# Ten unread transposes of the identity in each step of a graph-attention kernel

## The chip, the cores and the metric

The kernel runs on one core of one Trainium2 chip, as one launch. The metric is the device time of that launch in microseconds; lower is better.

## The reference

One layer of graph attention over 12500 nodes of 256 features and 200000 edges, sorted by destination, with 8 heads of 32:

```python
h = relu(layernorm(x))
q, k, v = h @ Wq + bq, h @ Wk + bk, h @ Wv + bv          # 8 heads of 32
logits = einsum('ehd,ehd->eh', q[dst], k[src]) / sqrt(32)
expv = exp(logits - segment_max(logits, dst)[dst])
attn = expv / segment_sum(expv, dst)[dst]
agg = segment_sum(attn[:, :, None] * v[src], dst)
y = h + gelu(agg + h @ Wskip + bskip)
out = x + layernorm(y) * gamma + beta
```

All arrays are float32.

## The kernel before

The kernel first normalises all nodes and writes two tables to memory, h and the joined keys and values (`kv_tab`, line 349 makes them). It also plans the edges: they are cut into 8 streams, and each stream into tiles of 128 edges. From about 250 us on, a loop over steps `c` does the edges; each step handles three tiles (`K = 3`) of each of the 8 streams (`S = 8`), 3072 edges. There are 64 steps. The loop has 63 passes, `c` from 0 to 62; 62 of them run the full body, and the last, `c == NST - 2`, takes a branch of its own and leaves the loop, and the work after it ends the kernel.

What one step does, with the lines of the profile:

- `gather` and `gather_row` (L1492, L1504): GpSimd fetches the rows of `kv_tab` of the edges' sources, one indirect DMA for each tile and stream.
- `windows`, `turn_windows` (L1466 transposes, L1470 copy) and `queries` (L1480, L1484, copy L1487): the rows of h of the destinations, turned, and multiplied by Wq, give the queries of the nodes.
- `hot_e` (matmul L1529, activation L1532) and `hot_n` (L1542, L1545): matrices of ones and zeros that say which edge belongs to which node, in the two directions.
- `spread` (L1555): TensorE spreads the nodes' queries over the edges, into PSUM. `times` (L1566) multiplies them by the keys on VectorE, `total` (L1573) sums over each head: the logits, 64 for each of 128 edges.
- `turn` (L1592): TensorE transposes a tile's logits into a bank of PSUM. `maxima` scans them in both directions for the maximum of each node (L1604, L1605), subtracts it (L1607) and takes exp on ScalarE (L1608). `turn_back` (L1614) transposes the three tiles of weights back.
- `weights` (L1626, L1629) copies the weights of tiles 1 and 2; `weigh` (L1640, L1646) multiplies the values by the weights on VectorE.
- `add_up` (L1663): TensorE sums the weighted values of each node, for three groups of streams; ScalarE copies the sums (L1676), carries the last node's on to the next step's tile (L1680), and SyncE stores them (L1686).
- A `Pair` of node blocks (L1197 to L1320) is finished beside the steps from step 15 on: skip connection, gelu, layer norm, output. The object `Dense` (L1823 to L1878) takes, from step 2 to 50, the edges whose destination is among the first 16 nodes, without gathers; its `turn` is L1831, its `back` L1862.

The order of instructions on each engine is the order in which the program writes them: `keep` hangs each instruction behind the one before it on the same engine, without a semaphore. `turns`, called right after certain matmuls, issues the next waiting gather behind the latest TensorE instruction, with a wait for it:

```python
def turns(behind, n=1):
    for _ in range(n):
        if waiting:
            gather_row(*waiting.pop(0), behind)
```

The bank of the logits is one tile for all steps but the last, of 128 partitions by 512 columns:

```python
logits = xt_ps.tile([P, 512], F32, name="ps_x")

def weight(c, j):
    at = (0, K * P, K * P + SH)[j]
    return step[c]["xt"][:, at:at + SH]
```

`turn` writes partitions 0 to 63 of columns 0 to 383, one tile of 128 columns at a time; the forward scan writes partitions 64 to 127 of the same columns. `turn_back` writes all 128 partitions of columns 0 to 63 (tile 0), 384 to 447 (tile 1) and 448 to 511 (tile 2); `SH` is 64.

The order of the work around the two places of the change: before `turn_back(c)` come, on TensorE, the third tile's `turn(c, 2)`, the dense part's `logits`, the rest of `add_up(c - 1, 0)`, `add_up(c - 1, 1)`, `pair.turn()` and `add_up(c - 1, 2)`; behind it `hot_n(c, 0)`, `hot_n(c, 1)` and `spread(c + 1, 1, 0)`. The last TensorE work of a step is `spread(c + 1, 2, 1)`, `hot_e(c + 2, 2)`, the first two tiles of `add_up(c, 0)` and `hot_e(c + 2, 3)`; the next step begins there with the dense part's `turn`, `shifted` of the pair before (L1299, L1302), two spreads, `turn_windows(c + 2, 0)` and the turn of the third tile.

At the kernel's start 18 transposes of the identity are issued in the same way (L281, `WARM = 18`), ahead of the first work of TensorE.

Of the kernel before, what the change touches and what calls it, by code (L numbers as in the profile page):

```python
# [44 lines left out]
P = 128  # L45
# [6 lines left out]
K = 3  # L52
# [18 lines left out]
SIDE, FOUR = 2, 4  # L71
ONCE = (2, 51)
START, WARM = 4, 18
LANDED, GATHERED, ASIDE, LATER = 2, 4, 12, 14
PAD = 127.0

# [7 lines left out]
def gnn_kernel(ctx: ExitStack, tc: tile.TileContext, x, src, dst, Wq, bq, Wk, bk, Wv, bv,  # L84
# [380 lines left out]
    with tc.If(fits > 0) as branch:  # L465
        table = dram.tile([S, NT, SUMS], F32, name="table")
        walk_streams(tc, N, HID, NST, KL, many, ident, idx, d0_row, slot_row, near, near_n, e_tab, pen_tab,
                     h_tab, kv_tab, table, x, out, w_q, w_s, one_row, b_q3, b_s3, b_o3,
                     gam, beta, eps, run_tab, cnt_tab, own, Wk, bk, Wv, bv)
# [643 lines left out]
def walk_streams(tc, N, HID, NST, KL, many, ident, idx, d0_row, slot_row, near, near_n, e_tab, pen_tab, h_tab,  # L1113
# [7 lines left out]
    nc = tc.nc  # L1121
# [15 lines left out]
    def behind(ins, name):  # L1137

        tc.add_manual_dep(ins.ins, name, mybir.DependencyInfo(
            mybir.DependencyClass.NoSync, mybir.DependencyReason.DATA), reason="kept order")  # L1140

    def keep(ins):

        before = latest.get(ins.ins.engine)
        if before is not None:
            behind(ins, before)
        latest[ins.ins.engine] = ins.ins.name
        return ins
# [231 lines left out]
    with ExitStack() as es:  # L1380
# [41 lines left out]
        def tiles_of(c):  # L1422
            return KL if c == NST - 1 else K
# [14 lines left out]
        def penalties(c):  # L1438

            g = step[c]  # L1440
            g["pen"] = early.tile([P, CH + 1], BF16, name="pen", bufs=2)
            keep(nc.sync.dma_start(g["pen"], bass.AP(
                tensor=pen_tab.tensor, offset=pen_tab.offset + c * 2 * S * (CH + 1),
                ap=[[CH + 1, 2 * S], [0, HEADS], [1, CH + 1]])))
# [66 lines left out]
# [5 lines that stand above are left out]
# [8 lines left out]
        def hot_e(c, i):  # L1524

            if i == 0:
                step[c]["to_e"] = hot.tile([P, S // 2, CH], F32, name="to_e")
            ps = hot_ps.tile([P, S * WN], F32, name="ps_hot")
            keep(nc.tensor.matmul(ps[:, :CH], near[:, i * P:(i + 1) * P], step[c]["et"],  # L1529
                                  start=True, stop=True))  # L1530
            turns(latest[PE], (1, 0, 0, 2)[i])
            keep(nc.scalar.activation(step[c]["to_e"][:, i, :], ps[:, :CH], AF.Relu, scale=-1.0,  # L1532
                                      bias=ones))

        def hot_n(c, j):

            n = near_n.shape[1]
            if j == 0:
                step[c]["to_n"] = (hot.tile([P, K, n], F32, name="to_n", bufs=1) if c < NST - 1
                                   else done[0].spare(n)[:, None, :])  # L1540
            ps = hot_ps.tile([P, S * WN], F32, name="ps_hot")[:, :n]
            keep(nc.tensor.matmul(ps, step[c]["et"][:, j * P:(j + 1) * P], near_n, start=True,  # L1542
                                  stop=True))
            turns(latest[PE], (1, 0, 1)[j])
            keep(nc.scalar.activation(step[c]["to_n"][:, j, :], ps, AF.Relu, scale=-1.0,  # L1545
                                      bias=ones))
# [30 lines left out]

        logits = xt_ps.tile([P, 512], F32, name="ps_x")

        def weight(c, j):  # L1580

            at = (0, K * P, K * P + SH)[j]
            return step[c]["xt"][:, at:at + SH]
# [26 lines left out]
        def turn_back(c):  # L1610
            g = step[c]

            for j in range(tiles_of(c)):
                keep(nc.tensor.transpose(weight(c, j), g["W"][:, j * P:(j + 1) * P],  # L1614
                                         ident[:SH, :SH]))
# [5 lines left out]
        def weights(c, streams=slice(0, S)):  # L1621

            g = step[c]
            if "vw" not in g:
                products(c)
            keep(nc.scalar.copy(wden[c % 2][0:1, streams],  # L1626
                                g["kv"][0][0:1, streams, HID - HEADS:HID]))
            for j in range(1, tiles_of(c)):
                keep(nc.scalar.copy(g["vw"][j][:, :, :HEADS],  # L1629
                                    weight(c, j).rearrange("p (s h) -> p s h", s=S)))  # L1630

        def weigh(c, j, streams=slice(0, S), engine=None):
            g = step[c]
            t = g["vw"][j][:, streams]
            if engine:
                wj = t[:, :, :HEADS]
            else:
                engine = nc.vector
                wj = weight(c, j).rearrange("p (s h) -> p s h", s=S)[:, streams]
            keep(engine.tensor_tensor(  # L1640
                t[:, :, HEADS:].rearrange("p s (h d) -> p s h d", h=HEADS),
                wj[:, :, :, None].to_broadcast([P, t.shape[1], HEADS, D]),
                g["kv"][j][:, streams, HID:].rearrange("p s (h d) -> p s h d", h=HEADS),
                op=OP.mult))
            if j == 0:
                keep(engine.tensor_tensor(t[:, :, :HEADS], wj, wden[c % 2][:, streams],  # L1646
                                          op=OP.mult))
# [361 lines left out]
        for c in range(NST - 1):  # L2009
# [108 lines left out]
            if a:  # L2118
                a.top()
                a.exps()  # L2120
            turn_back(c)
            hot_n(c, 0)
            weights(c)
# [68 lines left out]
            add_up(c, 0, range(K - 1))  # L2192
            penalties(c + 2)
            hot_e(c + 2, 3)
            before, pair = pair, pair_next
            if c > 1:
                step[c - 2] = None
# [484 lines left out]
```

## Time and profile before

| | |
|---|---|
| time, median of 3 runs | 2711.11 us (2701.12 to 2712.65) |
| the profiled execution's own time | 2722.66 us |
| its span, first to last instruction | 2721.1 us |
| mean granted TensorE clock | 0.833 |
| busy: TensorE, VectorE, ScalarE, GpSimd | 77%, 70%, 44%, 58% of the span |
| transfers | 589.91 MB, mean 217 GB/s |

In the lines of the profile, PE is TensorE's matmuls, PEld its weight loads, DVE VectorE, ACT ScalarE, POOL GpSimd and SP SyncE. A row of a group gives the line of the kernel, the engine, the operation, the tiles written and read with their shapes, the number of instructions, then the busy time, the mean duration of one in ns, and the idle time of that engine just before these instructions with what ended it. A row in order of time gives the start, the duration, the same names, and in brackets the idle time before it. A row of waits gives the waiting instruction, what released it, the sum in us, how often, and the longest. A row of a stretch gives its length, then the busy time and number of instructions of PE, PEld, DVE, ACT and POOL, the granted clock of TensorE (1.00 is full), the busy share of the DMA engines, and GB/s. "issue" stands where the profile shows nothing that was waited for.

### The profile page before, as it was taken

To read this page: it belongs to the slowest core of one execution; us is meant where nothing else is said; L and a number is where in the kernel's file an instruction comes from. 1 tells how busy PE (TensorE), PEld (TensorE's weight loads), DVE (VectorE), ACT (ScalarE), POOL (GpSimd) and SP (SyncE) were. 2 spreads that over 40 slices of the span, in tenths; PEclk is the share of its full clock that TensorE was granted. 3 is DMA by queue.
4 is the path that set the end of the run, shared out by engine and by line. 5 is a ranking of instruction groups with operands and counts; after the bars stand their busy time and mean duration, and the time that the engine had idled before them with its cause. 6 is when DMAs were issued, how large, how long until landed. Compare 5 with 4: busy or idle time off the path is not lost. (4 is left out here: it accounts for less than half of the span.)

```text
span 2721.1 us, 38398 instructions
## 1 busy us (share of the span) xinstructions
PE 2093.9 (77%) x10881; PEld 1272.9 (47%) x10881; DVE 1915.3 (70%) x2373; ACT 1204.8 (44%) x2789; POOL 1591.6 (58%) x1744
## 2 busy tenths in 40 slices
PE   9994667776777778877878877787887777767776
PEld 4443444444444445544544444454554444444444
DVE  8885666666676667767766776666777766777776
ACT  5652233332334445445444544444545444444444
POOL 5457466666666556555555655555555555666664
PEclk9997688888788788878887887878888878887778
DMA  9777566766767677767777777767777776777774
GB/s 351 293 273 220 155 200 207 211 206 207 204 209 214 204 215 224 214 208 232 220 210 206 224 213 208 221 204 207 224 221 212 224 213 203 220 225 222 222 214 113
DMA packets 275205, 589.91 MB, mean 217 GB/s; under 512 B 60643, under 2 KB 133400, under 8 KB 272038
## 3 DMA queue, kind: packets, MB, share of 16 engines
q0 software_dynamic: 125344, 409.89, 51.4%
q1 hardware_dynamic: 148416, 176.36, 20.5%
q8 instruction: 89, 1.46, 0.2%
q10 hardware_dynamic: 1222, 1.11, 0.1%
q14 instruction: 134, 1.10, 0.1%
HBM read 505.52 MB, written 81.63 MB: 216 GB/s over the span
## 5 line engine op out<-in xcount | busy, mean ns | idle before, releaser
L1504 POOL DMA_INDIRECT kv<-kv_tab,idx x1472 | 1401.8, 952 | 981.9 <-issue 335.9
L1555 PE MATMUL ps_qe<-qw,to_e 64*128 64x256 f32 x3040 | 589.3, 501 | 34.1 <-DVE kv L1566 25.4
L1566 DVE TENSOR_TENSOR kv<-ps_qe,kv 128x1024 f32<-128x1024 f32 x380 | 451.5, 1217 | 147.2 <-remote 91.4
L1555 PEld LDWEIGHTS ps_qe<-qw,to_e 64*128 64x128 f32 x3040 | 403.5, 249 | 126.6 <-issue 45.5
L1640 DVE TENSOR_TENSOR vw<-ps_x,kv 128x2048 f32<-128x2048 f32 x188 | 427.0, 2271 | 49.7 <-ACT vw L1629 16.6
L1573 DVE TENSOR_REDUCE L<-kv 128x64 f32<-128x2048 f32 x190 | 433.9, 2283 | 4.8
L1484 PE MATMUL ps_hot<-w_q,hwT 128*128 128x256 f32 x768 | 251.3, 475 | 18.5 <-issue 9.9
L1663 PE MATMUL ps_a<-vw,to_n 128*32 128x264 f32 (+1 forms) x2232 | 228.4, 435 | 44.6 <-issue 25.3
L1532 ACT ACTIVATE to_e<-ps_hot,ones 128x384 f32<-128x384 f32 x256 | 146.9, 581 | 255.1 <-remote 96.9
L1487 ACT COPY qw<-ps_hot 128x256 f32<-128x256 f32 (+1 forms) x128 | 60.6, 474 | 344.0 <-PE ps_hot L1484 113.4
L1484 PEld LDWEIGHTS ps_hot<-w_q,hwT 128*128 128x128 f32 x768 | 165.6, 230 | 86.3 <-ACT hwT L1470 34.0
L1663 PEld LDWEIGHTS ps_a<-vw,to_n 128*32 128x32 f32 (+1 forms) x2232 | 88.7, 125 | 245.9 <-issue 194.3
L349 PE MATMUL ps_kv<-w_kv,hT 128*128 128x512 f32 x392 | 184.3, 593 | 0.7 <-ACT hT L263 0.7
L1420 ACT ACT_TABLE_LOAD x142 | 182.2, 1283 | 2.6
L1529 PE MATMUL ps_hot<-et,near 48*128 48x384 bf16 x256 | 94.1, 368 | 102.1 <-issue 84.8
L1614 PE MATMUL ps_x<-ident,W 64*128 64x64 f32 x189 | 28.9, 270 | 179.4 <-ACT hT L1222 113.9
L1470 ACT COPY hwT<-ps_hot 128x256 f32<-128x256 f32 (+1 forms) x128 | 61.2, 478 | 233.7 <-PE ps_hot L1466 129.5
L1604 DVE TENSOR_TENSOR_SCAN ps_x<-pen,ps_x 64x384 f32<-64x384 bf16 x63 | 60.6, 961 | 147.6 <-PE ps_x L1592 79.2
L1866 DVE TENSOR_TENSOR kv<-ps_hot,kv 128x256 f32<-128x256 f32 x49 | 20.8, 425 | 181.1 <-PE ps_hot L1862 100.3
L1680 ACT COPY kv<-ps_a 1x264 f32<-1x264 f32 x372 | 137.3, 369 | 4.5
L1545 ACT ACTIVATE to_n<-ps_hot,ones 128x384 f32<-128x384 f32 x189 | 108.6, 576 | 62.8 <-PE ps_hot L1542 44.9
L1614 PEld LDWEIGHTS ps_x<-ident,W 64*128 64x128 f32 x189 | 19.2, 161 | 210.6 <-ACT hT L1222 132.0
(437 smaller groups left out, 3029.3 us busy)
## 6 DMA issues: line engine op xcount, KB each, us to landing
kv<-kv_tab,idx POOLq DMA_INDIRECT x1520
kv_tab<-kvo SPq DMA_DIRECT2D x23, 1024.0 KB
hw<-h_tab SPq DMA_DIRECT2D x256, 64.0 KB
table<-sums_w SPq DMA_DIRECT2D x252, 61.9 KB
kv<-h_tab SPq DMA_DIRECT2D x98, 128.0 KB
sums<-table SPq DMA_DIRECT2D x94, 132.0 KB
h<-h_tab SPq DMA_DIRECT2D x94, 128.0 KB
x_f<-in_x_dram SPq DMA_DIRECT2D x94, 128.0 KB
```

The lines of the kernel that those rows point to most:

```text
L349: nc.tensor.matmul(ps_kv, hT[:, c, :], w_kv[:, c, :], start=c == 0, stop=c == KC - 1)
L1420: keep(nc.scalar.activation(dummy[:, 1:2], dummy[:, 0:1], function))
L1484: keep(nc.tensor.matmul(ps[:, b, :], g["hwT"][:, b, k, :], w_q[:, k, :], start=False, stop=k == KC - 1, skip_group_check=True))
L1504: ins = nc.gpsimd.indirect_dma_start(out=t[:, s, :], out_offset=None, in_=kv_tab[:, :], in_offset=bass.IndirectOffsetOnAxis(ap=idx[:, s, j ...
L1532: keep(nc.scalar.activation(step[c]["to_e"][:, i, :], ps[:, :CH], AF.Relu, scale=-1.0, bias=ones))
L1545: keep(nc.scalar.activation(step[c]["to_n"][:, j, :], ps, AF.Relu, scale=-1.0, bias=ones))
L1555: keep(nc.tensor.matmul(ps[:, b, a, :], g["to_e"][r, 2 * half + a, j * P:(j + 1) * P], g["qw"][r, (half + a) * half, :], start=True, stop= ...
L1566: keep(nc.vector.tensor_tensor(k, g["qe", half].rearrange("p b a d -> p a b d"), k, op=OP.mult))
L1573: keep(nc.vector.tensor_reduce(g["L"][:, j, :].rearrange("p (s h) -> p s h", s=S), g["kv"][j][:, :, :HID].rearrange("p s (h d) -> p s h d" ...
L1640: keep(engine.tensor_tensor(t[:, :, HEADS:].rearrange("p s (h d) -> p s h d", h=HEADS), wj[:, :, :, None].to_broadcast([P, t.shape[1], HEA ...
L1663: keep(nc.tensor.matmul(ps[at:at + w, :], g["to_n"][:, j, i * P + at:i * P + at + w], g["vw"][j][:, s, :], start=j == 0, stop=j == tiles_o ...
L1680: keep(copy(step[c + 1]["kv"][0][0:1, s, HID - HEADS:], ps[at:at + 1, :]))
```

## The change

A constant `IDLE = 5` and a function `idle(at, n)` are added. It issues `n` transposes of the 128 x 128 identity into columns `at` to `at + 127` of the bank of the logits, all 128 partitions. Nothing reads what they write. It is called twice in the loop's full body: with columns 384 to 511 ahead of `turn_back(c)`, and with columns 256 to 383 at the step's end, behind `hot_e(c + 2, 3)`. Both calls are in the body that the last pass leaves before. Nothing is removed or moved.

```diff
+IDLE = 5
...
         logits = xt_ps.tile([P, 512], F32, name="ps_x")
+
+        def idle(at, n):
+
+            for _ in range(n):
+                keep(nc.tensor.transpose(logits[:, at:at + P], ident, ident))
...
             if a:
                 a.top()
                 a.exps()
+            idle(K * P, IDLE)
             turn_back(c)
             hot_n(c, 0)
             weights(c)
...
             add_up(c, 0, range(K - 1))
             penalties(c + 2)
             hot_e(c + 2, 3)
+            idle((K - 1) * P, IDLE)
             before, pair = pair, pair_next
```

## The prediction

> **What bounds the kernel now.** I read the page's head first, then the groups by line, then stretches of time for the granted clock, then one step in order of time. The head says that no engine is full:
>
> ```profile
> span 2721.1 us, 38398 instructions
> PE 2093.9 (77%) x10881; PEld 1272.9 (47%) x10881; DVE 1915.3 (70%) x2373; ACT 1204.8 (44%) x2789; POOL 1591.6 (58%) x1744
> PEclk9997688888788788878887887878888878887778
> ```
>
> TensorE is the busiest, and its clock stands at seven to eight tenths after the first 200 us. Cutting the span into stretches of 3.4133 us, laid on the instants at which the clock changes, shows what the tenths are made of: each stretch is wholly at 1.00 or wholly at 0.50. The columns are the length, busy time of PE, PEld, DVE, ACT, POOL, then the clock.
>
> ```profile
> 1497.57:1500.99 3.42, 3.08 (x26) 1.57 (x22) 3.38 (x6) 1.34 (x4) 2.05 (x3) 1.00 0.73 232
> 1500.99:1504.40 3.41, 0.77 (x8) 0.75 (x10) 2.32 (x2) 2.82 (x9) 1.90 (x2) 1.00 0.67 191
> 1504.40:1507.81 3.41, 3.41 (x16) 2.33 (x14) 1.25 (x2) 2.70 (x9) 2.26 (x3) 0.50 0.71 209
> ...
> 1524.88:1528.29 3.41, 1.47 (x17) 0.70 (x10) 3.38 (x5) 0.80 (x2) 1.41 (x2) 1.00 0.85 275
> 1528.29:1531.71 3.42, 3.00 (x7) 1.66 (x8) 1.35 (x3) 2.31 (x6) 1.90 (x2) 0.50 0.47 122
> 1531.71:1535.12 3.41, 3.41 (x17) 2.24 (x16) 0.40 (x1) 0.00 (x0) 0.94 (x1) 0.50 0.34 100
> 1535.12:1538.53 3.41, 3.41 (x29) 1.92 (x28) 2.87 (x5) 2.11 (x6) 2.63 (x3) 1.00 0.65 171
> 1538.53:1541.95 3.42, 2.20 (x18) 1.19 (x16) 3.35 (x5) 1.36 (x5) 1.81 (x3) 1.00 0.76 237
> 1541.95:1545.36 3.41, 1.83 (x15) 1.33 (x15) 1.67 (x1) 3.34 (x12) 2.19 (x3) 1.00 0.65 182
> 1545.36:1548.77 3.41, 3.12 (x13) 2.19 (x12) 2.20 (x2) 1.98 (x4) 1.89 (x2) 0.50 0.77 235
> ...
> 1562.43:1565.84 3.41, 1.67 (x18) 0.51 (x17) 1.24 (x2) 1.16 (x2) 2.15 (x3) 1.00 0.82 252
> 1565.84:1569.25 3.41, 1.82 (x6) 1.05 (x7) 2.45 (x4) 1.62 (x5) 1.90 (x2) 0.50 0.68 195
> 262.00:2650.00 2388.00, 1817.24 (x9804) 1125.96 (x9805) 1663.75 (x1681) 1034.97 (x2408) 1405.15 (x1476) 0.82 0.72 212
> ```
>
> A full-clock stretch in which PE is busy for 0.77, 1.47, 1.83 or 1.67 us is followed by a half-clock one; after 2.20 us it is not. And half clock ends only after a stretch that is busy from end to end (3.41 of 3.41; after 3.00 it stayed). The same cut from 262 us on has 137 such falls (the first after 265.36, the last after 2630.80). Nineteen in twenty had under 1.85 us busy; of the 312 stretches after which the clock stayed full, the least busy twentieth begins below that. So the border lies near 1.5 to 1.8 us in 3.41. A clock of 0.82 over 2388 us is 2388 x 2 x 0.18 = 860 us at half clock, 6.3 us a fall, about two falls in each step of some 39 us.
>
> What half clock costs I take from whole steps, from one forward scan of the logits (L1604) to the next:
>
> ```profile
> 1177.61:1219.13 41.52, 33.79 (x170) 20.48 (x169) 28.34 (x31) 19.11 (x44) 22.52 (x24) 0.75 0.70 206
> 1413.39:1454.94 41.55, 33.66 (x170) 20.08 (x169) 28.33 (x31) 19.11 (x44) 23.03 (x24) 0.75 0.71 206
> 1296.48:1334.93 38.45, 30.19 (x170) 18.95 (x169) 28.32 (x32) 18.80 (x44) 22.42 (x25) 0.87 0.76 220
> 2014.75:2054.71 39.96, 30.64 (x170) 19.36 (x169) 28.27 (x32) 18.79 (x44) 22.96 (x25) 0.87 0.73 214
> ```
>
> The instructions are the same, 170 matmuls. At 0.75 a step has 41.5 x 0.5 = 20.8 us at half clock and takes 41.5 us; at 0.87 it has about 10.2 and takes 38.5 to 40.0, with 38.9 the mean of the twelve such steps between 858 and 2171 us. So (41.5 - 38.9) / (20.8 - 10.2) = 0.25 us of step for each us at half clock. PE is nearly always busy in half-clock stretches, so the most it could be is 0.5; half of the slowness reaches the step's end, half lies beside DVE, ACT and the gathers.
>
> **Where the two groups of transposes land.** PE alone, in order of time, one step:
>
> ```profile
> 1537.10 1.56 PE L1663 MATMUL ps_hot<-vw,to_n 128*64 128x264 f32 x12
> 1538.59 0.66 PE L1219 MATMUL ps_hot<-ident,h 128*128 128x128 f32 x4
> 1539.17 1.56 PE L1663 MATMUL ps_a<-vw,to_n 128*64 128x264 f32 x12
> 1543.18 0.40 PE L1614 MATMUL ps_x<-ident,W 64*128 64x64 f32 x3 [2.45 <-ACT hT L1222]
> ...
> 1525.41 0.33 PE L1529 MATMUL ps_hot<-et,near 48*128 48x384 bf16 x1
> 1525.69 0.66 PE L1831 MATMUL ps_hot<-ident,kv 128*128 128x128 f32 x4
> 1528.70 0.58 PE L1299 MATMUL ps_hot<-b_o,one_row 3*128 3x512 bf16 x1 [2.36 <-ACT to_e L1532]
> ```
>
> The group ahead of turn_back (call it A) follows the last L1663 of add_up(c - 1, 2) and stands in the wait of L1614. The one at the step's end (B) follows the last L1529 of hot_e(c + 2, 3) and stands ahead of L1831 (the dense part's turn) and L1299.
>
> **Price of a transpose.** The same instruction, identity into PSUM, stands at the kernel's start; L1219 and L1831 are the same form in the loop.
>
> ```profile
> 2.74 3.73 PE L281 MATMUL ps_t<-ident 128*128 128x128 f32 x18 [2.74 <-POOL ident masks.py:199]
> L281 PE MATMUL ps_t<-ident x18: 272/421/476, 2.7 to 6.2; 128*128 128x128 f32 x18
> L1614 PE MATMUL ps_x<-ident,W 64*128 64x64 f32 x189 | 28.9, 270 | 179.4 <-ACT hT L1222 113.9 <-issue 36.6 <-ACT W L1608 28.9
> PE ps_hot L1831 <- issue: 46.3, 22, 3.9
> PE ps_hot L1299 <- issue: 25.1, 18, 3.0
> PE ps_hot L1831 <- DMA hw<-h_tab: 15.3, 7, 2.6
> PE ps_hot L1299 <- ACT to_e L1532: 11.9, 7, 3.4
> ```
>
> Four L1219 take 0.66 us, one alone 0.27 (the least that L281 shows), so the second to fourth start 0.13 us apart on average; 0.11 where nothing holds the weight load. The L281 group, mostly at half clock, runs 18 in 3.73: 0.2 each. Five thus cost 0.55 us at full clock and 1.05 at half. The loop's full body runs for 62 steps (the last pass leaves before either place): 620 transposes, 620 weight loads.
>
> **Group A** is costed at nothing: L1614 waits 179.4 us in all, some 3 us a step, for exp(W) on ACT (behind the copy of L1222), and 0.55 to 1.05 us fits into it. Without that cover it would be 62 x 0.55 = 34 us. Its columns, 384 to 511, were last read by weigh(c - 1, 2) and by the copies of L1629, for which the matmuls of add_up just before it have waited, so no new wait for VectorE arises; turn_back writes them next, on the same engine.
>
> **Group B** delays whatever PE does next. The four rows of waits above are 54 waits and 98.6 us, mean 1.8, so in about 54 of 62 steps there is a wait, ahead of L1831 or right behind it ahead of L1299, that takes up the 0.55 us. In the other 8 the delay goes on to the spreads (L1555) and the turn of the last tile (L1592), for which the scan L1604 waits: 8 x 0.55 = 4.4 to 8 x 1.05 = 8.4 us, taken as 8, since the step's end is often at half clock. With no cover it would be 34 to 65 us. Its columns, 256 to 383, were last read by L1607 half a step earlier. No gather is hung on these transposes: the gathers' turns are taken from a matmul issued right before each call, and none of those calls follows either group directly. SP, POOL and ACT issue nothing new. PE's instruction stream grows by 1240 on some 21,800; I see no wait that I can put on its fetch.
>
> **What it saves.** The transposes add busy time at the front of both gaps. In the stretches quoted: B at 1525.74 to 1526.3, with L1831 pushed behind it into the gap, brings 1.47 to 2.0 us, above the border, so the 6.8 us at half clock from 1528.29 would go. B at 1564.8 brings 1.67 to 2.2. But A begins at 1500.66, of which 0.2 us falls into the stretch with 0.77: it stays below. And A at 1540.7 falls into the stretch that was busy enough already. The fall after 1514.64 (0.69 us busy) is of a third gap, ahead of L1466, that gets nothing. I did this for every stretch from 300 to 2650 us, pushing what follows B until a gap takes it up. With the border anywhere from 0.37 to 0.43 of a stretch, 11 to 16 of 135 falls rise above it; with a border of 0.46 to 0.5, 6 to 8. I take 16, as a stretch that climbs over the border is mostly one where the clock would have recovered late. 16 x 6.3 us x 0.25 = 25 us; by the most that half clock can cost (0.5), 50 us; with 6 falls, 9 us.
>
> **Sum.** -25 + 8 + 0 = -17 us. The profiled execution took 2722.66 us (span 2721.1), so 2705; the median of the runs, 2711.11, is 11.5 lower, so 2694. One chosen border decides a third of this. A change of 0.5% is 13.6 us, about what a measurement of this kernel can tell from none.
>
> [...] In the first stretch of the kernel PE runs nothing but transposes (L281), and their durations fall from 476 ns to 272 within the group, with nothing else on PE: transposes open the clock here. [...]
>
> **Rivals.**
> (1) *Nothing is saved.* Either transposes open the clock but do not hold it, or each fall that is avoided comes back one gap later, for instance in the third gap, or PE's regained time ends in DVE's and the gathers' waits. For it: some 120 of 137 falls are untouched even by my count, and the spread between steps at 0.87 (38.45 and 39.96) is as large as what one fall is worth. Against: the regular 41.5 us of every step at 0.75. Time: 2711 + 0 to 8, 2715.
> (2) *Slower, by group A: late reports of PE's work.* ACT's copy of the sums of add_up(c - 1, 1) needs the twelve L1663 that end at 1538.66, and starts only when the later L1663, which it doesn't need, are through:
>
> ```profile
> 1541.06 0.38 ACT L1676 COPY sums_w<-ps_hot 128x264 f32<-128x264 f32 x1 [2.01 <-PE ps_a L1663]
> 1542.12 0.59 ACT L1222 COPY hT<-ps_hot 128x512 f32<-128x512 f32 x1
> 1542.61 0.52 ACT L1608 ACTIVATE W<-W 64x384 f32<-64x384 f32 x1
> ...
> 1535.50 1.08 PE L1848 MATMUL ps_hot<-kv,keys 128*128 128x256 f32 x4
> 1536.62 0.48 ACT L1850 ACTIVATE pin<-ps_hot,less_b 128x256 f32<-128x256 f32 x1 [0.77 <-PE ps_hot L1848]
> ```
>
> If a matmul's completion is told only once PE's queue has run dry, five transposes behind the last L1663 put it off by 0.55 us, and the chain L1676, L1680, L1222, exp, turn_back is what the step waits for. That is 62 x 0.55 = 34 us: 2694 + 34 = 2728, or 2745 with nothing saved. It decides from 0.3 us a step on. Against: in the same step L1850 starts 0.04 us after L1848 ends, though more matmuls stand behind it.
> (3) *The saving is larger.* Faster steps have shorter gaps, and then further falls vanish by themselves; 16 falls at 0.5 and no loss at B give 2661.
>
> **How the numbers follow.** The forecast, (3) included: 0.50. Rival (1): 0.29. Rival (2): 0.21. Predicted time 2694. The forecast's own range is 2655 to 2706. With (1) whole and the near end of (2) the range is 2655 to 2733; only the far end of (2) and steps that lock into a new rhythm lie outside. Faster by over 0.5%: 0.48, a little less than the forecast, as its weak end (9 us saved) is no change; within 0.5%: 0.31; slower: 0.21.
>
> **What would show it.** Mean clock in the loop up from 0.82 to about 0.84, and falls down from 137 to about 120; those that vanish lie behind B, not A. L1614 starts no later after its exp than now. L1831 and L1299 wait less by about 0.5 us each step, and L1592 comes no later. Wrong if the falls stay at 137 (rival 1), if L1676 on ps_hot starts half a microsecond later after its own L1663 (rival 2), or if L1604 waits longer for L1592 (B without cover).

## The result and the profile after

The changed kernel takes 2825.61 us (median of 4 runs, 2820.89 to 2832.45) against 2711.46 us (median of 4 runs of the kernel before): ratio 1.0409, 95% interval 1.0367 to 1.0451. It is 114 us slower, 1.8 us in each of 62 steps. The forecast was 2694.

The profile of the changed kernel, head and three groups of its page (the transposes are L1584; lines behind them have moved by 6, and weigh's L1640 is now L1646):

```profile
span 2819.3 us, 39698 instructions
PE 2164.2 (77%) x11501; PEld 1328.0 (47%) x11501; DVE 1905.2 (68%) x2373; ACT 1209.9 (43%) x2789; POOL 1594.0 (57%) x1744
L1646 DVE TENSOR_TENSOR vw<-ps_x,kv 128x2048 f32<-128x2048 f32 x188 | 428.5, 2280 | 588.0 <-PE ps_hot L1837 327.6
L1556 PE MATMUL ps_qe<-qw,to_e 64*128 64x256 f32 x3040 | 581.4, 501 | 172.6 <-DVE kv L1567 169.8
L1584 PE MATMUL ps_x<-ident 128*128 128x128 f32 x620 | 105.0, 305 | 2.7 <-DVE W L1613 2.7
```

In the profile of before, weigh and the spread had these rows:

```profile
L1640 DVE TENSOR_TENSOR vw<-ps_x,kv 128x2048 f32<-128x2048 f32 x188 | 427.0, 2271 | 49.7 <-ACT vw L1629 16.6
L1555 PE MATMUL ps_qe<-qw,to_e 64*128 64x256 f32 x3040 | 589.3, 501 | 34.1 <-DVE kv L1566 25.4
...
1521.46 0.30 DVE L1258 BATCH_NORM_AGGREGATE mv<-st 128x2 f32<-128x6 f32 x2
1521.68 2.26 DVE L1640 TENSOR_TENSOR vw<-ps_x,kv 128x2048 f32<-128x2048 f32 x1
```

The transposes cost what was expected: 620 of them, 105 us of PE's time, hardly a wait of their own. What is new stands two rows above: VectorE was idle for 49.7 us ahead of weigh and is now idle for 588.0 us. In order of time, after:

```profile
1619.40 0.30 DVE L1259 BATCH_NORM_AGGREGATE mv<-st 128x2 f32<-128x6 f32 x2
...
1624.60 0.33 PE L1530 MATMUL ps_hot<-et,near 48*128 48x384 bf16 x1
1624.87 0.77 PE L1584 MATMUL ps_x<-ident 128*128 128x128 f32 x5
1628.55 1.01 PE L1837 MATMUL ps_hot<-ident,kv 128*128 128x128 f32 x4 [2.92 <-issue]
1630.29 2.29 DVE L1646 TENSOR_TENSOR vw<-ps_x,kv 128x2048 f32<-128x2048 f32 x1 [10.58 <-PE ps_hot L1837]
1632.49 2.35 DVE L1567 TENSOR_TENSOR kv<-ps_qe,kv 128x1024 f32<-128x1024 f32 x2
1633.76 3.06 PEld L1556 LDWEIGHTS ps_qe<-qw,to_e 64*128 64x128 f32 x16 [2.39 <-DVE kv L1567]
```

Before, weigh(c, 2) began as soon as VectorE was through with the statistics of the pair, while TensorE was still at the end of its step. Now VectorE stands still from 1619.7 to 1630.29, until 4.65 us after the end of group B (1624.87 + 0.77). The row names L1837, the first work behind B, as what ended the wait. Late starts of this kind are found on this chip elsewhere too (a copy 3.2 us behind its matmuls, against 0.4 on another chip, in the last section). On the chips of the experiments the row names the transposes themselves, and in the step shown below weigh starts 0.04 us after the fifth. Then times (L1567) is late, and the spread (L1556) that needs the PSUM freed by times is late, with 172.6 us of idle time ahead of it in place of 34.1: TensorE and VectorE take turns where they had worked side by side.

Group B writes columns 256 to 383 and weigh(c, 2) reads columns 448 to 511, but of one bank, which is one tile of the program. With B ahead of it there, weigh waits although the columns differ: 588.0 us of idle time here, 365.6 and 384.9 in two of the runs below, against 8.4 where the transposes go to another bank.

### The profile page after: what moved, and what is told of

It is laid out like the page before. It is cut to its first block, busy times and chain, and to the rows that moved or that the text cites. A ratio compares the mean times of both kernels' runs of the same rounds, so it can differ in the third digit from the quotient of the medians.

```text
span 2819.3 us, 39698 instructions
## 1 busy us (share of the span) xinstructions
PE 2164.2 (77%) x11501; PEld 1328.0 (47%) x11501; DVE 1905.2 (68%) x2373; ACT 1209.9 (43%) x2789; POOL 1594.0 (57%) x1744
## 5 line engine op out<-in xcount | busy, mean ns | idle before, releaser
L1646 DVE TENSOR_TENSOR vw<-ps_x,kv 128x2048 f32<-128x2048 f32 x188 | 428.5, 2280 | 588.0 <-PE ps_hot L1837 327.6
L1556 PE MATMUL ps_qe<-qw,to_e 64*128 64x256 f32 x3040 | 581.4, 501 | 172.6 <-DVE kv L1567 169.8
L1556 PEld LDWEIGHTS ps_qe<-qw,to_e 64*128 64x128 f32 x3040 | 389.8, 247 | 290.6 <-DVE kv L1567 213.5
L1567 DVE TENSOR_TENSOR kv<-ps_qe,kv 128x1024 f32<-128x1024 f32 x380 | 446.6, 1216 | 17.3 <-remote 9.8
L1485 PE MATMUL ps_hot<-w_q,hwT 128*128 128x256 f32 x768 | 264.8, 495 | 22.4 <-issue 17.1
L1669 PE MATMUL ps_a<-vw,to_n 128*32 128x264 f32 (+1 forms) x2232 | 217.4, 419 | 6.8 <-issue 4.6
L1485 PEld LDWEIGHTS ps_hot<-w_q,hwT 128*128 128x128 f32 x768 | 175.1, 243 | 86.8 <-issue 34.3
L1273 ACT ACTIVATE sums<-sums,nm,rstd 128x256 f32<-128x256 f32 x92 | 50.2, 593 | 162.9 <-DVE nm L1268 160.8
L1598 PE MATMUL ps_x<-ident,L 128*64 128x128 f32 x189 | 59.7, 316 | 68.0 <-issue 46.5
L1238 PE MATMUL ps_a<-w_s,hT 128*128 128x256 f32 x368 | 107.2, 442 | 0.0
L1584 PE MATMUL ps_x<-ident 128*128 128x128 f32 x620 | 105.0, 305 | 2.7 <-DVE W L1613 2.7
```

The costliest lines, as they stand in the source:

```text
L1485: keep(nc.tensor.matmul(ps[:, b, :], g["hwT"][:, b, k, :], w_q[:, k, :], start=False, stop=k == KC - 1, skip_group_check=True))
L1556: keep(nc.tensor.matmul(ps[:, b, a, :], g["to_e"][r, 2 * half + a, j * P:(j + 1) * P], g["qw"][r, (half + a) * half, :], start=True, stop= ...
L1567: keep(nc.vector.tensor_tensor(k, g["qe", half].rearrange("p b a d -> p a b d"), k, op=OP.mult))
L1646: keep(engine.tensor_tensor(t[:, :, HEADS:].rearrange("p s (h d) -> p s h d", h=HEADS), wj[:, :, :, None].to_broadcast([P, t.shape[1], HEA ...
L1669: keep(nc.tensor.matmul(ps[at:at + w, :], g["to_n"][:, j, i * P + at:i * P + at + w], g["vw"][j][:, s, :], start=j == 0, stop=j == tiles_o ...
```

## The experiments

The runs below were taken on three chips, where the kernel before takes 2181 to 2187 us in place of 2711; they are taken to be others than the first (more on that at the end). Each ratio is to the kernel before, run beside it on the same chip. For the first chip there is only the trace above.

**Group A alone.**

```diff
-            idle((K - 1) * P, IDLE)
```

> The group ahead of turn_back alone (A), the group at the step's end (B) left out. Theory W (the loss is one wait: B writes the bank that weigh(c, 2) on VectorE has still to read, so VectorE begins each step by waiting for TensorE's end of the step before): 2690 to 2720 us, as before, idle time of VectorE ahead of weigh back from 588 us to about 50. Rival P (ten transposes delay TensorE's own chain, half of them each): about 2768. Rival A (the five transposes push back the reports of add_up and with them turn_back): 2800 or more.

Measured: 2187.86 us, ratio 0.9998 (0.9984 to 1.0012). The absolute times expected belong to the first chip; the ratio is theory W's. Idle time ahead of weigh is 10.0 us. Group A costs nothing and brings nothing that shows. Rival A, late reports, falls for this chip; the first chip is taken up below.

**Group B with a single transpose, no A.**

```diff
-            idle(K * P, IDLE)
...
-            idle((K - 1) * P, IDLE)
+            idle((K - 1) * P, 1)
```

> No group A; B with one transpose in place of five. Theory W: the wait is the same whether one or five are waited for, less 0.45 us a step of transposes: 2780 to 2825 us, VectorE's idle time ahead of weigh still above 450 us. Rival P: a tenth of the transposes, a tenth of the loss, about 2723. Rival A: as before, 2711.

Measured: 2386.71 us, ratio 1.0893 (1.0831 to 1.0955): one transpose of 0.11 us in a step costs 3.2 us a step. Its profile names what ended the wait:

```profile
L1646 DVE TENSOR_TENSOR vw<-ps_x,kv 128x2048 f32<-128x2048 f32 x188 | 428.4, 2279 | 365.6 <-PE ps_x L1584 365.6
```

Rival P, that TensorE's own time is the loss, is out: a tenth of the transposes cost 8.9%, of the 10.4% that all of them cost on such a chip (next run). The sizes expected were missed: 2780 to 2825 us is a ratio of 1.025 to 1.042, and the idle time was to stay above 450 us. Both were read from the first chip; here the wait is shorter and the loss larger.

**The changed kernel and the kernel before on one chip.**

> The changed kernel, unchanged, on the chip of this call. Theory W (VectorE's weigh(c, 2) waits for group B): at least the loss of B with one transpose, 3.2 us a step on the faster chip, more by the 0.45 us of four further transposes: ratio 1.085 to 1.12 on a chip where the kernel before takes 2190 us, 1.04 where it takes 2710. Rival P (TensorE's own time): a ratio of 1.02 at most, since A alone cost nothing.

> The kernel before, unchanged, profiled on the chip of this call, so that the others have their own trace to stand against. All theories: its time is that of the kernel before on this chip; on the chip of the first runs it was 2711 us, on that of the second call 2187.

Measured: 2405.38 against 2181.46 us, ratio 1.1037 (1.1009 to 1.1064), within theory W's range. The kernel before, its group of weigh, and in order of time the start of weigh(c, 2) in one step:

```profile
L1640 DVE TENSOR_TENSOR vw<-ps_x,kv 128x2048 f32<-128x2048 f32 x188 | 426.7, 2270 | 9.3 <-PE ps_x L1592 9.0
...
1208.77 0.30 DVE L1258 BATCH_NORM_AGGREGATE mv<-st 128x2 f32<-128x6 f32 x2
1208.98 2.26 DVE L1640 TENSOR_TENSOR vw<-ps_x,kv 128x2048 f32<-128x2048 f32 x1
...
1212.70 0.33 PE L1529 MATMUL ps_hot<-et,near 48*128 48x384 bf16 x1
1212.96 0.66 PE L1831 MATMUL ps_hot<-ident,kv 128*128 128x128 f32 x4
```

And the changed kernel, the same group and the same place:

```profile
L1646 DVE TENSOR_TENSOR vw<-ps_x,kv 128x2048 f32<-128x2048 f32 x188 | 428.2, 2278 | 384.9 <-PE ps_x L1584 384.9
...
1216.85 0.30 DVE L1259 BATCH_NORM_AGGREGATE mv<-st 128x2 f32<-128x6 f32 x2
...
1222.06 0.33 PE L1530 MATMUL ps_hot<-et,near 48*128 48x384 bf16 x1
1222.32 0.76 PE L1584 MATMUL ps_x<-ident 128*128 128x128 f32 x5
1222.92 0.60 PE L1837 MATMUL ps_hot<-ident,kv 128*128 128x128 f32 x4
1223.12 2.29 DVE L1646 TENSOR_TENSOR vw<-ps_x,kv 128x2048 f32<-128x2048 f32 x1 [5.97 <-PE ps_x L1584]
```

Here the order is plain: weigh began 3.7 us ahead of the last L1529, and now begins 0.04 us after the fifth transpose ends. From one to five transposes (and A, which is free) the ratio goes from 1.0893 to 1.1037, 31 us or 0.13 us for each further transpose of group B. The two intervals allow 0.07 to 0.19, and the two runs were on different chips; it fits the 0.11 us that a transpose takes on TensorE.

**The wait taken away at the reader: weigh(c, 2) from SBUF, with and without the transposes.**

```diff
-                weigh(c - 1, K - 1)
+                weigh(c - 1, K - 1, engine=nc.vector)
```

> Both groups as in the change, but weigh(c, 2) reads its weights from the copy that ScalarE has made in SBUF (L1629 of the kernel before) in place of the logits' bank, so nothing has to wait for B. Theory W: the loss goes: 2680 to 2715 us, VectorE's idle time ahead of weigh below 100 us. Rival P and rival A: 2800 to 2830, since all transposes are still there.

> The control of the run with both groups: the kernel before, with weigh(c, 2) reading its weights from SBUF, and no transposes. Theory W: 2695 to 2715 us, as before. The difference from the run with both groups is then what the transposes do alone, without the wait: by the forecast's clock -17 us for the transposes, by the rival that nothing is saved 0 to +8.

Measured: with both groups 2303.04 us, 1.0532 (1.0515 to 1.0550); without any 2294.76 us, 1.0494 (1.0476 to 1.0512). The idle time ahead of weigh is gone in both, and both groups of transposes together cost 8 us, 0.36%, where the forecast's clock would have given 17 us back. But the expected level was missed by 5%: the control itself is slow, for a reason of its own. In the control, VectorE and GpSimd in order of time:

```profile
1228.64 0.95 POOL L1504 DMA_INDIRECT kv<-kv_tab,idx  x1 [0.30 <-issue]
1229.26 2.26 DVE L1640 TENSOR_TENSOR vw<-vw,kv 128x2048 f32<-128x2048 f32 x1
1229.89 2.44 POOL L1504 DMA_INDIRECT kv<-kv_tab,idx  x1 [0.30 <-issue]
1231.43 1.22 DVE L1566 TENSOR_TENSOR kv<-ps_qe,kv 128x1024 f32<-128x1024 f32 x1
1232.64 0.95 POOL L1504 DMA_INDIRECT kv<-kv_tab,idx  x1 [0.30 <-DMA kv<-kv_tab,idx]
```

A gather issued while weigh reads both operands from SBUF takes 2.44 us in place of 0.95. One gather in each step is stretched past 1.5 us (61 of them, none in the kernel before), and their total grows from 1401.5 us (group A alone, on the same chip) to 1514.6, by 113 us. GpSimd's idle time (span less busy) stayed near what it was, 585 us against 593, so these 113 us fit the 107 us that the control lost; no run takes the stretching away alone. The gather that starts while weigh runs ends at 1232.33, 0.81 us after weigh. The weigh itself, which began while the gather before it still ran, takes its usual 2.26 us and shows no such delay. In the kernel before, where weigh reads its weights from PSUM, the gather issued at 1209.33, beside the weigh of 1208.98, takes 0.95 us. What stretches the gather was not shown. So this pair removes the wait but brings in another cost, and only their difference speaks on the transposes.

**The wait taken away by order: weigh(c, 2) written ahead of group B.**

```diff
             if c:
-                weigh(c - 1, K - 1)
                 gather_next(c - 1, K - 1)
...
             hot_e(c + 2, 3)
+            if c < NST - 3:
+                weigh(c, K - 1)
             idle((K - 1) * P, IDLE)
```

> Both groups, with weigh(c, 2) written ahead of group B in place of behind it (it stays VectorE's first work behind the statistics, and reads PSUM as before), so that VectorE does not wait for B; B waits for that read instead. Theory W: the wait of VectorE goes, ratio 0.99 to 1.01, and weigh's idle time is below 60 us; if TensorE then waits for VectorE at B, up to 1.03. Rival P: as the changed kernel, 1.04 to 1.12.

Measured: 2186.53 us, ratio 1.0025 (1.0012 to 1.0038). All 620 transposes are there, into the same columns, and 10.1% of the 10.4% is gone. Its groups:

```profile
L1646 DVE TENSOR_TENSOR vw<-ps_x,kv 128x2048 f32<-128x2048 f32 x188 | 426.7, 2270 | 7.8 <-PE ps_x L1598 7.8
L1584 PE MATMUL ps_x<-ident 128*128 128x128 f32 x620 | 95.8, 286 | 2.7 <-DVE W L1613 2.7
```

The same order without any transpose, and with B alone:

> weigh(c, 2) written at the step's end, and no transposes at all: the control of the runs with weigh(c, 2) ahead of B. The order on each engine is that of the kernel before, so 0.998 to 1.002 by all theories; more would mean that the moved read, not the transposes, carries the 0.2% that those runs lost.

> weigh(c, 2) ahead of group B, and no group A: B alone, without the wait. By the prediction it is B behind which falls of the clock vanish. Where the kernel before takes 2180 us: 1.000 to 1.004, with B's five transposes carrying most of the 5 us that both groups cost. Where it takes 2710 us: 0.985 to 0.997 by the prediction's clock, 1.000 to 1.004 by the rival that nothing is saved.

Measured: 1.0004 (0.9991 to 1.0018) and 1.0017 (1.0005 to 1.0029). The moved read shows no cost; B's five transposes, without the wait, cost some 3 us, though the two intervals overlap.

**Another bank.** No A; five transposes into free columns of the bank that add_up(c, 0) fills next, ahead of it:

```diff
+        def idle(c, n):
+            step[c]["bank"] = ag_ps.tile([P, 2 * HID], F32, name="ps_a")
+            for _ in range(n):
+                keep(nc.tensor.transpose(step[c]["bank"][:, SUMS:SUMS + P], ident, ident))
...
+                              g["bank"] if i == 0 and "bank" in g else
                               ag_ps.tile([P, 2 * HID], F32, name="ps_a"))[:, :SUMS]
...
+            idle(c, IDLE)
             add_up(c, 0, range(K - 1))
```

> No A; five transposes a step into free columns (264 to 391) of the bank that add_up(c, 0) fills next, issued just ahead of it, 1.4 us of TensorE's work earlier than B. That bank has no reader on VectorE or ScalarE before add_up is complete. Theory W: the loss is the bank, not the five transposes: ratio 0.99 to 1.01. Rival P: 1.04 or more.

Measured: 2191.46 us, 1.0044 (1.0026 to 1.0062). The group of weigh:

```profile
L1647 DVE TENSOR_TENSOR vw<-ps_x,kv 128x2048 f32<-128x2048 f32 x188 | 426.7, 2270 | 8.4 <-PE ps_x L1599 8.0
```

The transposes are still ahead of weigh in the program, but in another bank, and of the loss of some 10% only 0.4% is left. They stand 1.4 us of TensorE's work earlier than B. That alone would not have freed weigh, which began 3.7 us ahead of the matmul behind which B stands. So it takes both: the bank that weigh reads, and a place ahead of weigh in the program. The bank of the logits is also one tile of the program, so no run here tells an order by bank from an order by tile.

**What the clock is worth without the wait: 15 transposes in each group.**

```diff
-IDLE = 5
+IDLE = 15
```

> As the kernel with weigh(c, 2) ahead of group B, with 15 transposes in each group in place of 5: 30 a step. If time at half clock were worth 0.25 us of step each us, as the prediction took it: where the kernel before takes 2180 us it has 322 us at half clock, 5 a group brought that to 288, and 15 should bring it under 200, a ratio of 0.98 or less. If the clock is off the path there and each further transpose only costs TensorE's time: 20 more transposes of 0.11 us in 62 steps, 136 us if all were on the path, by the 5 us that the first ten cost about 10 to 40 us, a ratio of 1.005 to 1.02. Where the kernel before takes 2710 us, with 912 us at half clock: 0.95 to 0.98 by the first, 1.00 to 1.02 by the second.

> The kernel with weigh(c, 2) ahead of group B and 5 transposes in each group, as the partner of the one with 15 on the same chip. Where the kernel before takes 2180 us: 1.0025 as measured. Where it takes 2710 us: by the prediction's clock without the wait 0.985 to 0.997 (17 us saved), by the rival that nothing is saved 1.000 to 1.005.

Measured: 5 a group 1.0019 (1.0009 to 1.0030), 15 a group 2218.85 us, 1.0176 (1.0141 to 1.0211). The clock column over the loop, for the kernel before and for 15 a group:

```profile
230.00:2110.00 1880.00, 1591.91 (x9889) 995.46 (x9887) 1669.56 (x1697) 1043.67 (x2422) 1423.92 (x1492) 0.93 0.91 272
```

```profile
230.00:2130.00 1900.00, 1728.23 (x11621) 1157.47 (x11620) 1650.89 (x1681) 1034.74 (x2391) 1409.71 (x1481) 0.96 0.90 267
```

With 15 a group the clock stands at 0.96 in place of 0.93: over the whole kernel 200 us at half clock against 322. And the kernel got slower by 37 us. Against 5 a group it is 33 us for 1240 more transposes, about a quarter of 0.11 us for each. Some of TensorE's added time reaches the path: the forward scan of the logits waits longer for TensorE's turn. The first row is of the kernel before, the second of 15 a group:

```profile
L1604 DVE TENSOR_TENSOR_SCAN ps_x<-pen,ps_x 64x384 f32<-64x384 bf16 x63 | 60.4, 959 | 30.9 <-PE ps_x L1592 30.9
```

```profile
L1610 DVE TENSOR_TENSOR_SCAN ps_x<-pen,ps_x 64x384 f32<-64x384 bf16 x63 | 60.6, 962 | 79.9 <-PE ps_x L1598 79.9
```

The run shows the balance of the two effects, not each of them: what the higher clock gave back can't be told from what the transposes took. In the kernel before, on this chip, VectorE is busy for 87% of the span and the DMA engines for 91% of the loop, which suggests that TensorE's clock had little to give there.

## Why the prediction was wrong

**The step that failed is the one on group B's columns.** The prediction said: "Its columns, 256 to 383, were last read by L1607 half a step earlier." It asked who had used these columns before, and so whether TensorE would have to wait. It did not ask who still reads the bank behind B in the program. That is weigh(c, 2), written at the start of the next step. The wait then runs the other way: VectorE waits for TensorE, at the place where VectorE had run ahead. So the sum held 8 us for group B, for TensorE's delay alone, and nothing for the wait of VectorE ahead of weigh, which grew from 49.7 to 588.0 us on the first chip and from 9.3 to 384.9 on another.

The trace of the kernel before held a sign of it. Of the three weighs of a step, weigh(c, 2) alone waits there for a count that TensorE's matmuls raise. The latest TensorE write to the bank ahead of it in the program is turn(c + 1, 1), into columns 128 to 255, which it doesn't read. That write was nearly always done in time, so the row among the waits is small:

```profile
DVE vw L1640 <- PE ps_x L1592: 3.2, 5, 1.7
```

The change put a later write in its place. For group A the same question came out right, since turn_back, just behind it, writes the bank anyway and everything that reads it later waits for turn_back.

**The size.** On the first chip weigh's wait grew by 588.0 - 49.7 = 538 us, and VectorE's whole idle time (span less busy) only from 805.8 to 914.1, by 108. The other 430 us were given back where VectorE had waited elsewhere in the step, 328 of them in three groups. Before:

```profile
L1566 DVE TENSOR_TENSOR kv<-ps_qe,kv 128x1024 f32<-128x1024 f32 x380 | 451.5, 1217 | 147.2 <-remote 91.4 <-PE ps_hot L1529 39.1 <-PE ps_qe L1555 9.5
L1604 DVE TENSOR_TENSOR_SCAN ps_x<-pen,ps_x 64x384 f32<-64x384 bf16 x63 | 60.6, 961 | 147.6 <-PE ps_x L1592 79.2 <-PE ps_qe L1555 27.2 <-remote 15.4
L1866 DVE TENSOR_TENSOR kv<-ps_hot,kv 128x256 f32<-128x256 f32 x49 | 20.8, 425 | 181.1 <-PE ps_hot L1862 100.3 <-PE ps_qe L1555 56.5 <-issue 16.9
```

And after:

```profile
L1567 DVE TENSOR_TENSOR kv<-ps_qe,kv 128x1024 f32<-128x1024 f32 x380 | 446.6, 1216 | 17.3 <-remote 9.8 <-PE ps_qe L1556 5.4 <-PE ps_a L1750 2.2
L1610 DVE TENSOR_TENSOR_SCAN ps_x<-pen,ps_x 64x384 f32<-64x384 bf16 x63 | 60.3, 957 | 31.5 <-PE ps_x L1598 31.5
L1872 DVE TENSOR_TENSOR kv<-ps_hot,kv 128x256 f32<-128x256 f32 x49 | 20.8, 425 | 99.4 <-PE ps_hot L1868 65.1 <-PE ps_hot L1543 20.2 <-issue 10.3
```

On the chip where the changed kernel was run again, VectorE had only 275 us of idle time to give back (2181.3 less 1905.9), and the wait of 385 us cost 224. A shorter wait cost more, on the fuller engine.

**Price of a transpose:** right. 105 us for 620 on the first chip, 95 to 96 on another; 0.11 us from start to start, on the median.

**Group A at nothing:** right where it was run alone (0.9998), though not by the cover that was named. In the kernel before on such a chip, L1614 waits 22.5 us in all in place of 179.4, and still no cost shows:

```profile
L1614 PE MATMUL ps_x<-ident,W 64*128 64x64 f32 x189 | 25.1, 240 | 22.5 <-ACT W L1608 20.9 <-ACT hT L1222 1.4
```

On the first chip A was not run alone.

**Group B without the wait:** 4.4 to 8.4 us expected, about 3 measured on other chips (1.0017 less 1.0004, of 2181 us), not clear of noise.

**The saving of 25 us by the clock:** not found. With the wait out of the way, every run with group B was slower than the kernel before, by 0.2 to 1.8%. The price of 0.25 us a step for each us at half clock came from comparing slow with quick steps, which doesn't tell a step that is slow by its clock from one whose clock is low by its waits; that the clock is the cause was argued, never shown. The 15-a-group run doesn't refute the price either: at 0.25, its 122 us less of half clock would give 30 us back, which a cost of 67 us for 1860 transposes would hide. On the first chip, with nearly three times the half-clock time, the transposes were run only together with the wait. The clock of the loop went from 0.82 to 0.83 and the falls from 137 to 130, where 0.84 and about 120 were expected. What they would bring there without the wait stays open. One reading of the clock was too strict: of the 137 half-clock stretches after which full clock came back, the least busy had 2.97 us of 3.41, not all of it.

**The rivals.** That nothing is saved, on balance, is what the runs without the wait show on the other chips. The slower rival, late reports behind A, is not borne out: on the first chip the copy L1676 started on the median 3.2 us after its own L1663 in the kernel before, and 1.9 us after it in the changed one, where half a microsecond more was expected. So this rival had the right sign by luck: its mechanism is another, and its price of 34 us was a third of the loss.

**Transposes and the clock.** The prediction read from L281 that transposes open the clock. The runs have the same sign: with 15 a group the clock of the loop is 0.96 against 0.93, and the whole kernel has 200 us at half clock against 322.

## What to carry to other kernels

In this kernel, unused columns of the bank of the logits were not free space: one transpose a step into columns that weigh(c, 2) doesn't read, ahead of it in the program, made the kernel 8.9% slower. So list the readers of the bank that come behind the write, not only those before it. The places that cost little here were ahead of a point where the other engines wait for TensorE anyway (turn_back, 0.9998), behind the last read of the bank (weigh moved ahead of B, 1.0025), and in a bank that only TensorE touches until its next real result (1.0044). And whether holding a clock pays is to be taken from an experiment, not from a comparison of slow and quick steps.

## What the runs showed of the hardware that was not expected

The same program takes 2711 us where it was run first and 2181 to 2187 us on three chips later, which were alike to 0.3%. The first chip has no number on record; that it is a fourth one is taken from its time. The instructions are the same, the waits differ: the copy L1676 of the second sums, first chip, then one of the three:

```profile
L1676 ACT COPY sums_w<-ps_hot 128x264 f32<-128x264 f32 x64 | 24.2, 379 | 147.7 <-PE ps_a L1663 88.6 <-remote 58.9
```

```profile
L1676 ACT COPY sums_w<-ps_hot 128x264 f32<-128x264 f32 x64 | 24.1, 379 | 3.0 <-PE ps_hot L1663 1.6
```

On the first chip it starts 3.2 us (median) after the matmuls that it needs, on the other 0.4 us. So, by these traces, what waits for TensorE's work started later after it on the first chip. Much of the idle time of TensorE that the prediction read goes with it: L1614's wait is 179.4 us there and 22.5 us on the other, and half clock 912 us against 322. What causes the delay was not tried.
